# An elementwise add moved from GpSimd to an accumulating DMA, with a second buffer for its tile and VectorE's operations in another order

## The chip, the core and the metric

The kernel runs on one core of a Trainium2 chip. The metric is the time of one execution on the device in microseconds (us). It is given as the median of three runs, and a profiled execution shows where the time goes. The engines are TensorE (PE, with its weight loads as PEld), VectorE (DVE), ScalarE (ACT) and GpSimd (POOL); SyncE (SP) issues the loads and stores.

## The reference

128 samples of 64 channels and 1024 positions pass through four style-modulated 1-D convolutions with three taps (plain, upsampling by two, plain, downsampling by two), with blurs, and the input is added at the end:

```python
s = style @ mw.T + mb
weight = SCALE * w * s[:, None, :, None]
demod = lax.rsqrt(jnp.sum(weight * weight, axis=(2, 3)) + EPS)
weight = weight * demod[:, :, None, None]
...
x = x + _L0_cond_ref(x, cond_512, L0_cond_weights, ...)
```

All four layers and both blurs are linear, so each sample has one 64x64 filter with nine taps of its own, and a constant per channel. At the sequence's ends the four layers are done one by one (Ye, Ue, Ve, Oe).

## The kernel before, in words

Everything is float32. Two samples fill the 128 partitions; four samples make a quad, 32 quads in all. For each quad the kernel composes the nine taps on TensorE in stages (`stage1`, `stage2`, `stage3`, each with a scaled copy by ScalarE), and `combine_a` and `combine_b` on VectorE turn them into the filters `W` (tiles Wf) and `H` of a short convolution with five products. The nine-tap filter is three groups of three taps; the input's three planes, every third position each (344 columns), are combined into five inputs T0 to T4, and five products `conv0` to `conv4` (24 matmul instructions each, 340 columns) give three output planes.

The inputs of a quad, from its loaded tile X (both pairs of samples, three planes) and a work tile G of the same shape:

- `in_g2` (VectorE, line L712, 128x684) writes plane 2 of G, and `in_g01` (VectorE, L712, 128x1376) planes 0 and 1.
- `in1` (L776) writes T1 = plane 2 + plane 1 of G, `in2` (L781) T2 = plane 2 - plane 1. Both run on GpSimd from turn 1 on.
- `in04` (VectorE, L790, 128x1368) writes T0 and T4 from all three planes of G.
- `in3` (VectorE, L761) writes T3 from X alone.

G has one buffer, so the next quad's `in_g2` comes after all readers of the last quad's G. T tiles have two buffers, X two, and the PSUM pool `ps_w`, which the composing stages share, one. Y is a PSUM tile of its own; its spare columns also hold small sums of the constants, and a `memset` (L1524) clears them in turns 1 to 6 (`SMALL`).

The schedule is written out by hand: each engine runs its instructions in program order, and the tile framework adds the semaphores. After a set-up, four turns `early_turn(0)` to `early_turn(3)`, then `turn_of(q)` for q = 4 to 28, then the last quads in line. `turn_of(q)` works on several quads at once: it composes c = q + 2 (stages 2 and 3) and s = q + 4 (stage 1), ends the products of q and begins those of n = q + 1. Turn 4 is the entry (`entry`), with its own order. The products of a turn come in the order conv2(q), conv4(q), conv3(n), conv0(q), conv1(n) on TensorE. Between them:

- `r_sums` (L638, GpSimd) sums columns of the tile R that ScalarE has just copied out of stage2's PSUM.
- `sum2(q)` on VectorE (L712, Y from m and psA, then L862) follows conv2 and writes Y, on which conv4 accumulates; `sum1(n)` (L712, y from psA and m) follows conv1.
- `stage1_b(s)` has matmuls, then two operations of VectorE (L481, S from psS, one for each half), then a sum of S on GpSimd (L484).
- `share_sums` (L501) and `share_copy` (L529, ScalarE) prepare part of the next turn's stage2 in the `ps_w` bank; turn 5 is without them, and its stage2 is all matmuls (L589).
- `SIDE` and `LATE` hold side work of VectorE, one item a turn: set-up of tables and constants, and the sequence ends (for example `setup1`, L1016).

The profile's own lines name TensorE's matmuls by helper: L803 the products, L506 and L589 stage2, L621 stage3, L428 stage1, L1044 the ends, L1295 the constants.

Of the kernel before, what the change touches and what calls it, by code (L numbers as in the profile page):

```python
# [48 lines left out]
F32 = mybir.dt.float32  # L49
AF = mybir.ActivationFunctionType  # L50
ALU = mybir.AluOpType
# [12 lines left out]
def kernel(  # L64
# [10 lines left out]
    NP, P, NXC = x.shape  # L75
    B = 2 * NP
    NQ = B // 4
# [5 lines left out]
    nc_v, nc_a, nc_g = nc.vector, nc.scalar, nc.gpsimd  # L83
# [3 lines left out]
    const = ctx.enter_context(tc.tile_pool(name="const", bufs=1))  # L87
# [4 lines left out]
    wf_pool = ctx.enter_context(tc.tile_pool(name="wf_pool", bufs=3))  # L92
    tpool = ctx.enter_context(tc.tile_pool(name="tpool", bufs=2))
    mpool = ctx.enter_context(tc.tile_pool(name="mpool", bufs=1))
    gpool = ctx.enter_context(tc.tile_pool(name="gpool", bufs=1))
    opool = ctx.enter_context(tc.tile_pool(name="opool", bufs=2))
    ps_conv = ctx.enter_context(tc.tile_pool(name="ps_conv", bufs=2, space=PSUM))
    ps_w = ctx.enter_context(tc.tile_pool(name="ps_w", bufs=1, space=PSUM))
# [39 lines left out]
    PL = NXC // 3  # L138
# [27 lines left out]
    def unit(pool, name):  # L166

        if pool is ps_w:
            return [pool.tile([P, 512], F32, tag=f"u{r}", name=f"{name}_{r}") for r in range(2)]
        t = pool.tile([P, 2, 512], F32, tag="u", name=name)  # L170
        return [t[:, r, :] for r in range(2)]


    NB = 340
# [266 lines left out]
    def flat(t):  # L441
        return t.rearrange("c a o -> c (a o)")
# [117 lines left out]
    def stage2(q, pool=None, engs=(nc_a, nc_a), between=None):  # L560
        if q in shared_ps:
            ps = stage2_rest(q)
        else:
            ps = opened.pop(q, None)
            taps = range(9) if ps is None else range(3, 9)
            ps = stage2_taps(q, taps, ps or unit(pool or ps_w, f"psR{q}"))
        if between:
            between()
        t = r_pool.tile([P, 2, 9, C], F32, tag="R", name=f"R{q}")
        for r in range(2):  # L570
            scaled_copy(engs[r], flat(t[:, r, :7]), ps[r][:, : 7 * C], tC[:, q, r : r + 1])
        chain[q] = t
        return ps
# [28 lines left out]
    def tap(kind, g):  # L602
        return range(9)[TAPS[kind]][g]
# [32 lines left out]
    def r_sums(q, eng):  # L636
        t = chain[q]
        eng.tensor_add(t[:, :, 7:9], t[:, :, 2:6:3], t[:, :, 3:7:3])  # L638
# [97 lines left out]
    Ts = {}  # L736
    Gs = {}
# [5 lines left out]
    def plane(buf, i, pairs=BOTH_PAIRS):  # L743

        at = PL * (2 - i) if i < 3 else PL * 2 + 1
        return buf[:, pairs, at : at + NJ]
# [11 lines left out]
    def in3(q, pairs=BOTH_PAIRS):  # L758
        if q < NQ:
            X, t = Xs[q % NX], t_tile(q, "T3")  # L760
            nc_v.tensor_sub(t[:, pairs, 0, :NJ], plane(X, 3, pairs), plane(X, 1, pairs))  # L761

    def in_g01(q, pairs=BOTH_PAIRS):
        if q < NQ:
            X, g = g_tile(q)
            sum_of(g[:, pairs, PL:], X[:, pairs, : 2 * PL], 0.5, X[:, pairs, PL:], ALU.subtract)

    def in_g2(q, pairs=BOTH_PAIRS):
        if q < NQ:
            X, g = g_tile(q)  # L770
            sum_of(plane(g, 2, pairs), plane(X, 3, pairs), 0.5, plane(X, 2, pairs), ALU.subtract)

    def in1(q, eng):
        if q < NQ:
            t, g = t_tile(q, "T12"), Gs[q]
            eng.tensor_add(t[:, :, 0, :NJ], plane(g, 2), plane(g, 1))  # L776

    def in2(q, eng):
        if q < NQ:
            t, g = t_tile(q, "T12"), Gs[q]  # L780
            eng.tensor_sub(t[:, :, 1, :NJ], plane(g, 2), plane(g, 1))  # L781

    def in04(q, pairs=BOTH_PAIRS):
        if q < NQ:
            t, g = t_tile(q, "T04"), Gs[q]
            a, b = g[:, pairs, :NJ], g[:, pairs, 2 * PL : 2 * PL + NJ]
            both = lambda v, step: bass.AP(
                v.tensor, v.offset, [*(list(d) for d in v.ap[:-1]), [step, 2], [1, NJ]]
            )
            nc_v.tensor_sub(t[:, pairs, :, :NJ], both(a, PL), both(b, 1))  # L790

    def product(q, m, ps, groups=range(K), alone=False):

        W, H_ = Wq[q]
        tag, i = SLOT[m]
        for g in groups:
            for s, rows in enumerate(HALF):
                for c, cols in enumerate(HALF):
                    if m in (0, 4):
                        w = W[rows, tap(m // 2, g), c, :]  # L800
                    else:
                        w = H_[rows, m - 1, g, c, :]
                    nc.tensor.matmul(  # L803
                        ps[s][cols, :NB],
                        w,
                        Ts[q, tag][rows, c, i, g : g + NB],
                        start=(g == 0 and (m == 3 or alone)),
                        stop=(g == K - 1),
                        skip_group_check=True,
                    )  # L810
# [36 lines left out]
    def sum1(q):  # L847

        y1w[q] = m_tile("y1", q, 2)
        for s, a in parts(q):  # L850
            sum_of(y1w[q][:, s], a, 2.0, m3c[q][:, s])
# [4 lines left out]
    def sum2(q, steps=(0, 1)):  # L856
        if 0 in steps:
            m3 = m3c.pop(q)
            for s, a in enumerate(banks(q)):
                sum_of(Y[:, s, :NB], m3[:, s], 3.0, a[:, :NB])  # L860
        for s, a in parts(q) if 1 in steps else ():
            nc_v.tensor_sub(y1w[q][:, s], y1w[q][:, s], a)  # L862
# [4 lines left out]
    def conv0(q, *groups):  # L867
        product(q, 0, banks(q), groups)
# [18 lines left out]
            os[q][:, s, planes].rearrange("c i j -> c (i j)"),  # L887
        )


    raw = const.tile([P, 512], F32, name="raw")

    WIDE = 6
    ends_ps = {}
# [94 lines left out]
    g1 = const.tile([P, 6, C], F32, name="g1")  # L989

    Ye = [const.tile([P, HB, 8], F32, name=f"Ye{s}") for s in range(2)]
    Ue = [const.tile([P, HB, 11], F32, name=f"Ue{s}") for s in range(2)]
    Ve = [const.tile([P, HB, 12], F32, name=f"Ve{s}") for s in range(2)]
    Oe = const.tile([P, B, 3], F32, name="Oe")
# [33 lines left out]
    def setup1(part):  # L1028
        blurred(g1, woi[1], 0.25, 0.75, part)
# [248 lines left out]
    def high(n):  # L1278
        return Y[:, 1, NB + 4 : NB + 4 + n]
# [10 lines left out]
    def small(q):  # L1290
        l, bs = SMALL[q]
        dst = high(bs.stop - bs.start)
        src = c0f if l == 0 else cc[l - 1]
        for cols in HALF:
            nc.tensor.matmul(  # L1295
                dst[cols], wsum[T, l, :], src[T, bs], start=False, stop=True, skip_group_check=True
            )
# [26 lines left out]
    def last_factors():  # L1324
# [17 lines left out]
        11: lambda: add0(0),  # L1342
        12: lambda: add0(1),
        13: lambda: setup1(0),
        15: setup3,
        16: lambda: rest1_bias(0),
        17: lambda: rest1_bias(1),
# [7 lines left out]
        26: lambda: blur_side(0, 2),  # L1355
        27: lambda: blur_side(1, 2),
    }

    LATE = {13: lambda: setup1(1)}

    def extra(*at):
        EXTRA.get(at, lambda: None)()
# [1 line left out]
    def side(work, q):  # L1364
        work.get(q, lambda: None)()
# [117 lines left out]
    def turn_of(q):  # L1483
        n, c, s = q + 1, q + 2, q + 4
        entry = q == FIRST
        stage2(c)
        if entry:
            sum2(q)
            conv4(q)
            combine_a(n)  # L1490
            r_sums(c, nc_v)
        else:
            conv2(q)
            r_sums(c, nc_g)
            sum2(q)
            in2(n, nc_g)
        side(TABLES, q)
        for i in range(3):
            load(c + 1, slice(i, i + 1))
        stage3_b(c, open_a(n))  # L1500
        if entry:
            conv0(q, 0, 1)
        else:
            combine_a(n)
            conv4(q)
        stage3_a(c)
        combine_b(n)
        conv3(n)
        if entry:
            copy_m3(n)  # L1510
            stage1_a(s)
        outputs(q, 2)
        if not entry:
            if s < NQ:
                stage1_a(s)
            copy_m3(n)
        in04(n)
        if sharing(q):
            share_sums(c + 1)
        in_g2(c)  # L1520
        side(SIDE, q)
        if q in SMALL:
            l, bs = SMALL[q]
            nc_v.memset(high(bs.stop - bs.start), 0.0)  # L1524
        conv0(q, *((2,) if entry else range(K)))
        if entry:
            conv1(n, 0, 1)
        outputs(q, 1)
        if s < NQ:
            stage1_b(s)  # L1530
        in_g01(c)
        if sharing(q):
            share(c + 1, banks(q))
            share_copy(c + 1)
        outputs(q, 0)
        if q in SLOTS:
            matmuls, width, rest = SLOTS[q]
            slot(matmuls, width, Y_banks)
            rest()
        if s == NQ:  # L1540
            slot(ends3, 3, unit(ps_w, "psE"), 3)
            rest3()
        conv1(n, *((2,) if entry else range(K)))
        if q in SMALL:
            small(q)
        sum1(n)
        in3(c)
        side(LATE, q)
        if s == NQ:
            in04(c)  # L1550
        in1(c, nc_g)
        if s + 1 < NQ:
            scale3(s + 1)

# [3 lines left out]
        turn_of(q)  # L1558

    q, n, c = NQ - 3, NQ - 2, NQ - 1  # L1560
    stage2(c)
    conv2(q)
    in2(n, nc_g)
    stage3(c, 0)
    sum2(q, (0,))
    combine_a(n)
# [26 lines left out]
    q, n = NQ - 2, NQ - 1  # L1593
# [128 lines left out]
```

## Time and profile before

| | us |
|---|---|
| median of three runs | 475.28 |
| the three runs | 474.98, 475.28, 476.53 |
| span of the profiled execution | 475.5 |
| TensorE matmul, busy | 469.7 |
| VectorE, busy | 417.3 |
| ScalarE, busy | 312.0 |
| GpSimd, busy | 165.8 |

The profiled execution's own time is known only by its span, 475.5 us from the first to the last instruction. A timeline row reads: start, duration (of a merged group from the start of its first to the end of its last), engine, line, operation, output<-input, form, count, and in brackets the idle time before it with what ended it. A row of windows gives the stretch, its length, each engine's busy time with its number of instructions, the granted TensorE clock (1.00 is full), the busy share of the DMA engines and GB/s. A row of DMA issues gives the queue, the count, the size, and the median us from issue to landing.

### The profile page before, as it was taken

To read this page: it belongs to the slowest core of one execution; us is meant where nothing else is said; L and a number is where in the kernel's file an instruction comes from. 1 tells how busy PE (TensorE), PEld (TensorE's weight loads), DVE (VectorE), ACT (ScalarE), POOL (GpSimd) and SP (SyncE) were. 2 spreads that over 40 slices of the span, in tenths; PEclk is the share of its full clock that TensorE was granted. 3 is DMA by queue.
4 is the path that set the end of the run, shared out by engine and by line. 5 is a ranking of instruction groups with operands and counts; after the bars stand their busy time and mean duration, and the time that the engine had idled before them with its cause. 6 is when DMAs were issued, how large, how long until landed. Compare 5 with 4: busy or idle time off the path is not lost.

```text
span 475.5 us, 26771 instructions
## 1 busy us (share of the span) xinstructions
PE 469.7 (99%) x11932; PEld 349.5 (74%) x11932; DVE 417.3 (88%) x694; ACT 312.0 (66%) x711; POOL 165.8 (35%) x200
## 2 busy tenths in 40 slices
PE   9999999999999999999999999999999999999996
PEld 6987788777678876677776677766788787876653
DVE  3889998879989998899979899979998999999896
ACT  4565657577766676766667666667666777766464
POOL 3634033664444342233432233422333423243200
PEclk9999999999999999999999999999999999999999
DMA  5237456535445554345544454543555544455225
GB/s 176 71 115 224 150 151 180 152 113 177 139 145 166 166 166 136 123 150 169 163 150 126 130 168 152 178 124 121 152 164 169 164 145 147 148 152 161 80 91 193
DMA packets 52707, 70.71 MB, mean 149 GB/s; under 512 B 6000, under 2 KB 50672, under 8 KB 52592
## 3 DMA queue, kind: packets, MB, share of 16 engines
q1 hardware_dynamic: 52368, 68.78, 46.3%
q8 instruction: 93, 1.52, 1.4%
q10 hardware_dynamic: 224, 0.22, 0.1%
q14 instruction: 22, 0.18, 0.1%
HBM read 35.36 MB, written 33.62 MB: 145 GB/s over the span
## 4 chain that ended last, share of the span: by engine, by line
PE 99%; DVE 0%; ACT 0%; issue 0%
PE psA L803 47%; PE Y L803 12%; PE psR L506 9%; PE psW L621 7%; PE psA L621 7%; PE psS L428 6%; PE psR L589 5%; PE psA L506 2%; PE Y L1044 2%; PE Y L183 1%; PE Y L379 1%; PE psM L220 0%; PE psE L1044 0%; PE Y L255 0%; DVE o L882 0%; PE psM L255 0%
## 5 line engine op out<-in xcount | busy, mean ns | idle before, releaser
L803 PE MATMUL psA<-T,H 64*64 64x340 f32 x2304 | 185.9, 446 | 0.0
L803 PEld LDWEIGHTS psA<-T,H 64*64 64x64 f32 x2304 | 90.7, 133 | 46.9 <-issue 2.5
L712 DVE SCALAR_TENSOR_TENSOR G<-X 128x1376 f32<-128x1376 f32 (+2 forms) x65 | 78.0, 1206 | 0.2
L776 POOL TENSOR_TENSOR T<-G 128x684 f32<-128x684 f32 x28 | 46.3, 1652 | 73.7 <-DVE G L712 73.7
L484 POOL TENSOR_TENSOR S<-S 128x128 f32<-128x128 f32 x28 | 21.6, 772 | 139.7 <-ACT S L399 139.6
L399 ACT ACTIVATE R<-psR,tC 128x448 f32<-128x448 f32 x63 | 36.6, 631 | 43.6 <-PE psR L506 25.8
L803 PE MATMUL psA<-T,Wf 64*64 64x340 f32 x768 | 63.7, 446 | 0.0
L803 PE MATMUL Y<-T,Wf 64*64 64x340 f32 x768 | 62.4, 451 | 0.0
L712 DVE SCALAR_TENSOR_TENSOR Y<-m,psA 128x340 f32<-128x340 f32 x62 | 32.0, 516 | 28.2 <-PE psA L803 26.9
L399 ACT ACTIVATE psW<-psA 128x128 f32<-128x128 f32 x100 | 19.3, 268 | 49.1 <-PE psA L621 45.0
L790 DVE TENSOR_TENSOR T<-G 128x1368 f32<-128x1368 f32 (+1 forms) x33 | 50.8, 1541 | 0.0
L399 ACT ACTIVATE Wf<-psW,t 128x256 f32<-128x256 f32 (+2 forms) x76 | 32.7, 480 | 26.7 <-PE psW L621 26.4
L761 DVE TENSOR_TENSOR T<-X 128x684 f32<-128x684 f32 x32 | 47.7, 1492 | 0.0
L506 PE MATMUL psR<-S,E 64*64 64x64 f32 (+1 forms) x1472 | 46.8, 237 | 0.0
L781 POOL TENSOR_TENSOR T<-G 128x684 f32<-128x684 f32 x28 | 46.5, 1660 | 0.0
L428 PEld LDWEIGHTS psS<-wd,w2n 64*64 64x64 f32 x1120 | 35.1, 133 | 12.9 <-issue 0.3
L506 PEld LDWEIGHTS psR<-S,E 64*64 64x64 f32 x1472 | 39.5, 134 | 4.9 <-ACT psR L529 0.2
L803 PEld LDWEIGHTS Y<-T,Wf 64*64 64x64 f32 x768 | 30.3, 132 | 16.8
L803 PEld LDWEIGHTS psA<-T,Wf 64*64 64x64 f32 x768 | 29.8, 133 | 14.5
L880 ACT ACTIVATE o<-psA,tb,td 128x340 f32<-128x340 f32 x63 | 37.1, 648 | 5.0 <-PE psA L803 2.8
L880 ACT ACTIVATE o<-y,tb,td 128x340 f32<-128x340 f32 x62 | 38.5, 678 | 0.0
L880 ACT ACTIVATE o<-Y,tb,td 128x340 f32<-128x340 f32 x62 | 36.1, 639 | 2.8 <-PE Y L803 2.0
(180 smaller groups left out, 840.4 us busy)
## 6 DMA issues: line engine op xcount, KB each, us to landing
out<-o SPq DMA_DIRECT2D x191, 170.0 KB, 2.6
X<-in_x SPq DMA_DIRECT2D x150, 172.0 KB, 3.4
X<-in_x SPq DMA_DIRECT2D x14, 516.0 KB, 5.0
par<-in_params SPq DMA_DIRECT2D x3, 192.0 KB, 3.8
Xe<-in_x_ends SPq DMA_DIRECT2D x1, 512.0 KB, 4.5
out<-Oe SPq DMA_DIRECT2D x2, 96.0 KB, 2.1
out<-o ACTq DMA_DIRECT2D x1, 170.0 KB, 2.8
par<-in_params SPq DMA_DIRECT2D x1, 160.0 KB, 2.7
```

Of the source, the lines that this page charges most:

```text
L399: nc_a.activation(dst, src, AF.Copy, scale=f)
L428: nc.tensor.matmul(ps[r][cols, at * C : (at + n) * C], weight[rows], wd[c if r == 0 else 1 - c][rows, taps], start=first, stop=last, skip_ ...
L506: nc.tensor.matmul(dst[r][cols], weight[rows], st[c if r == 0 else 1 - c][rows, slots, :], start=False, stop=last, skip_group_check=True,)
L589: nc.tensor.matmul(ps[r][cols, lo * C : (lo + m) * C], E[rows, e + 2, :], src[rows, a, :], start=(n == 0), stop=(n == 8), skip_group_check ...
L621: nc.tensor.matmul(dst[r][cols], weight[rows], t[rows, c, slots, :], start=first, stop=last, skip_group_check=True,)
L712: nc_v.scalar_tensor_tensor(out, x, f, y, op0=ALU.mult, op1=op)
L761: nc_v.tensor_sub(t[:, pairs, 0, :NJ], plane(X, 3, pairs), plane(X, 1, pairs))
L776: eng.tensor_add(t[:, :, 0, :NJ], plane(g, 2), plane(g, 1))
L781: eng.tensor_sub(t[:, :, 1, :NJ], plane(g, 2), plane(g, 1))
L790: nc_v.tensor_sub(t[:, pairs, :, :NJ], both(a, PL), both(b, 1))
L803: nc.tensor.matmul(ps[s][cols, :NB], w, Ts[q, tag][rows, c, i, g : g + NB], start=(g == 0 and (m == 3 or alone)), stop=(g == K - 1), skip_ ...
L880: nc_a.activation(dst, src, AF.Identity, bias=add, scale=d3)
```

## The change

- G gets two buffers.
- A new `in1_dma(q)` replaces `in1` for quads 6 to 30. It issues a DMA from GpSimd's queue that adds plane 1 of G onto plane 2 in place, so T1 then lies in G itself, and conv1 of those quads reads it there (`first_of`). In a turn it is issued for n, behind `r_sums`. 
- `in2` moves from there to the end of the turn before, where `in1` was.
- `in04(n)` leaves the middle of the turn (but for the entry turn), and `in04(c)` stands at the end of each turn, between `sum1` and `in3`.
- `in_g2` and `in_g01` stand together, behind the side work and the memset, and ahead of stage 1's second half.
- `LATE` is gone: the second `setup1` is side work of turn 14.
- The tile `raw` lies over `Ye[0]` instead of having its own memory.
- In the last quads `in1_dma(30)` stands ahead of stage2, and `in2(30)` is gone from there.

```diff
-    gpool = ctx.enter_context(tc.tile_pool(name="gpool", bufs=1))
+    gpool = ctx.enter_context(tc.tile_pool(name="gpool", bufs=2))
...
+    def in1_dma(q):
+
+        g = Gs[q]
+        nc_g.dma_start(plane(g, 2), plane(g, 1), accum_op=ALU.add)
+        first_of[q] = g[:, :, :PL]
+
+    first_of = {}
+
...
+        if m == 1 and q in first_of:
+            src = first_of[q]
+        else:
+            src = Ts[q, tag][:, :, i]
...
-                        Ts[q, tag][rows, c, i, g : g + NB],
+                        src[rows, c, g : g + NB],
...
-    raw = const.tile([P, 512], F32, name="raw")
...
+    raw = Ye[0].rearrange("c b e -> c (b e)")
...
+        14: lambda: setup1(1),
...
-    LATE = {13: lambda: setup1(1)}
...
             r_sums(c, nc_g)
+            in1_dma(n)
             sum2(q)
-            in2(n, nc_g)
...
-        in04(n)
+        if entry:
+            in04(n)
         if sharing(q):
             share_sums(c + 1)
-        in_g2(c)
         side(SIDE, q)
         if q in SMALL:
             l, bs = SMALL[q]
             nc_v.memset(high(bs.stop - bs.start), 0.0)
+        in_g2(c)
+        in_g01(c)
         conv0(q, *((2,) if entry else range(K)))
...
         if s < NQ:
             stage1_b(s)
-        in_g01(c)
...
+        in2(c, nc_g)
         sum1(n)
+        in04(c)
         in3(c)
-        side(LATE, q)
-        if s == NQ:
-            in04(c)
-        in1(c, nc_g)
...
     q, n, c = NQ - 3, NQ - 2, NQ - 1
+    in1_dma(n)
     stage2(c)
     conv2(q)
-    in2(n, nc_g)
```

## The prediction

> **What bounds the kernel now.** I read the page's busy table and chain first, then the timelines of one late turn engine by engine, then the first turn of the late loop, then waits and DMA.
>
> ```profile
> span 475.5 us, 26771 instructions
> PE 469.7 (99%) x11932; PEld 349.5 (74%) x11932; DVE 417.3 (88%) x694; ACT 312.0 (66%) x711; POOL 165.8 (35%) x200
> PE 99%; DVE 0%; ACT 0%; issue 0%
> ```
>
> The chain that ended last is TensorE from end to end. So work taken off VectorE or GpSimd is worth nothing by itself, and the question is only whether some wait now reaches TensorE. TensorE's rows of turn 13 (first the end of turn 12, last the start of turn 14):
>
> ```profile
> 215.10 0.40 PE L506 MATMUL psR<-S,E 64*64 64x128 f32 x8
> 217.03 1.90 PE L803 MATMUL psA<-T,H 64*64 64x340 f32 x24
> 219.86 0.40 PE L621 MATMUL psA<-R,par 64*64 64x128 f32 x8
> 220.12 1.95 PE L803 MATMUL Y<-T,Wf 64*64 64x340 f32 x24
> 221.88 0.40 PE L621 MATMUL psW<-R,wsq 64*64 64x128 f32 x8
> 222.10 0.40 PE L621 MATMUL psW<-R,par 64*64 64x128 f32 x8
> 227.22 1.90 PE L803 MATMUL psA<-T,H 64*64 64x340 f32 x24
> 228.94 0.40 PE L506 MATMUL psR<-S,E 64*64 64x128 f32 x8
> ```
>
> 215.10 to 228.94 is one turn, 13.84 us: stage2, conv2 at 217.03, conv4 at 220.12, conv1 at 227.22. Back to back a product of 24 takes 1.72 (228.94 - 227.22). Eight of 64x128 go by in 0.22 (221.88 to 222.10), so behind those of 219.86 conv4 could start at 220.08; it starts 0.04 later and then takes 1.76 (221.88 - 220.12). That 0.08 is all that a turn could gain there.
>
> **The change, steady turns.** VectorE, GpSimd and one ScalarE row of the same stretch:
>
> ```profile
> 215.42 0.87 DVE L712 SCALAR_TENSOR_TENSOR y<-psA,m 128x680 f32<-128x680 f32 x1
> 216.21 1.81 DVE L761 TENSOR_TENSOR T<-X 128x684 f32<-128x684 f32 x1
> 219.00 1.07 DVE L712 SCALAR_TENSOR_TENSOR Y<-m,psA 128x340 f32<-128x340 f32 x2 [0.98 <-PE psA L803]
> 223.87 1.58 DVE L790 TENSOR_TENSOR T<-G 128x1368 f32<-128x1368 f32 x1
> 225.37 0.42 DVE L501 TENSOR_TENSOR S<-S 128x256 f32<-128x256 f32 x1
> 225.70 0.86 DVE L712 SCALAR_TENSOR_TENSOR G<-X 128x684 f32<-128x684 f32 x1
> 226.48 1.00 DVE L1016 SCALAR_TENSOR_TENSOR g<-par,g 128x192 f32<-128x192 f32 x2
> 227.41 0.60 DVE L481 SCALAR_TENSOR_TENSOR S<-psS,tB,S 128x128 f32<-128x128 f32 x2
> 227.92 1.58 DVE L712 SCALAR_TENSOR_TENSOR G<-X 128x1376 f32<-128x1376 f32 x1
> ```
>
> ```profile
> 215.64 1.65 POOL L776 TENSOR_TENSOR T<-G 128x684 f32<-128x684 f32 x1 [2.61 <-DVE G L712]
> 218.56 0.72 POOL L638 TENSOR_TENSOR R<-R 128x256 f32<-128x256 f32 x1 [1.27 <-ACT R L399]
> 226.05 0.82 POOL L484 TENSOR_TENSOR S<-S 128x128 f32<-128x128 f32 x1 [5.15 <-ACT S L399]
> ```
>
> ```profile
> 227.84 0.63 ACT L529 COPY psR<-psA 128x256 f32<-128x256 f32 x2
> ```
>
> Costs are start to start, since VectorE overlaps neighbours by some 0.08.
>
> *T0/T4 (in04, L790) out, first G part (in_g01, L712 128x1376) in, ahead of L481.* in04 is worth 225.37 - 223.87 = 1.50; in_g01 has the same 1.58 of duration, so 1.50 as well. So share_sums goes to 223.87, side to 224.20, in_g2 to 225.13, in_g01 to 225.91, and L481 stays at 227.41. That matters because L481 empties the PSUM bank that the copy L529 then fills for the next stage2: copy end 228.47 against stage2 at 228.94, 0.47 of cover. Net 0. L484 on GpSimd falls beside in_g01 now; at worst it holds VectorE for its own 0.82, and that is the one place where cover could run out by 0.35 in a turn; I take 0, since in_g01 starts first (225.91 against 226.05).
>
> *in04 ahead of in3, behind sum1.* sum1 waits for conv1: its end, 228.94, plus the 0.25 that sum2 shows behind conv2 (217.03 + 1.72 = 18.75, start 19.00), 229.19. Then 0.79 for sum1, in04 from 229.98 to 231.48, in3, and sum2 is due at 219.00 + 13.84 = 232.84. in3 has 1.36. It takes 1.81 now, beside GpSimd's add of in1; in turn 10, where other matmuls held sum1 back and that add was over:
>
> ```profile
> 188.52 0.86 DVE L761 TENSOR_TENSOR T<-X 128x684 f32<-128x684 f32 x1
> 191.32 1.07 DVE L712 SCALAR_TENSOR_TENSOR Y<-m,psA 128x340 f32<-128x340 f32 x2 [1.93 <-PE psA L803]
> ```
>
> At 0.86 it fits with 0.5 to spare; at 1.81 sum2, and conv4 behind it, are late by 0.45. GpSimd's in2 (1.65, the price of its twin L776) can start when in_g01 ends at 227.41 and L484 behind it at about 227.9, and ends at 229.55, before in04 at 229.98. So I take 0.86, and 0 for TensorE.
>
> *in1 as an accumulating DMA.* It leaves GpSimd's queue behind r_sums, at 218.56 + 0.72 = 219.28, with in2 and in04 of that quad done a turn's end before. Only the S sum at 226.05 queues behind it, which no one needs before the next turn. conv1 needs its 342 KiB at 227.22: 7.94 us. The second G buffer takes away the wait on conv1's reads. No DMA between SBUF tiles is in this trace, so bounds come from the loads:
>
> ```profile
> X<-in_x SPq DMA_DIRECT2D x150, 172.0 KB, 3.4
> out<-o SPq DMA_DIRECT2D x191, 170.0 KB, 2.6
> ```
>
> ```profile
> 221.28:222.28 1.00, 1.00 (x28) 0.70 (x24) 0.97 (x5) 0.72 (x2) 0.00 (x0) 1.00 0.90 279
> 222.28:223.28 1.00, 1.00 (x37) 0.73 (x32) 0.96 (x3) 0.35 (x1) 0.00 (x0) 1.00 0.10 37
> 224.28:225.28 1.00, 1.00 (x36) 0.77 (x32) 1.00 (x1) 0.69 (x3) 0.00 (x0) 1.00 0.08 31
> ```
>
> The second last column is the share of the DMA engines: full to 222.28 with the six X loads, then nearly idle. Low end 2.6 us, one store. High end: it starts only behind the X loads at 222.28, its three streams (two read, one written) cost three times two loads' bytes at 279 GB/s, 1.05 MB or 3.8 us, plus 3.4 to land: 229.5, which is 2.3 late. I take twice an X load, 6.8 us (the same rows of 1.4 KB, twice as many): 226.1, hidden by 1.1. [...]
>
> **The change, entry turn.** Turn 4 is different. Its VectorE rows:
>
> ```profile
> 96.37 0.87 DVE L712 SCALAR_TENSOR_TENSOR G<-X 128x684 f32<-128x684 f32 x1
> 100.74 0.14 DVE L1524 MEMSET Y<- 128x96 f32 x1 [2.39 <-ACT o L880]
> 100.79 0.53 DVE L481 SCALAR_TENSOR_TENSOR S<-psS,tB,S 128x128 f32<-128x128 f32 x2
> 101.23 1.58 DVE L712 SCALAR_TENSOR_TENSOR G<-X 128x1376 f32<-128x1376 f32 x1
> 102.73 0.86 DVE L712 SCALAR_TENSOR_TENSOR y<-psA,m 128x680 f32<-128x680 f32 x1
> ```
>
> ```profile
> 99.47 1.17 ACT L880 ACTIVATE o<-Y,tb,td 128x340 f32<-128x340 f32 x2
> ```
>
> ```profile
> 101.02 0.38 PE L1295 MATMUL Y<-c0f,wsum 64*64 64x96 f32 x4
> 101.21 2.71 PE L589 MATMUL psR<-S,E 64*64 64x192 f32 x70
> 103.92 1.88 PE L803 MATMUL psA<-T,H 64*64 64x340 f32 x22
> ```
>
> The memset of the spare columns of Y waits 2.39 us for ScalarE to have read Y (99.47 + 1.17 = 100.64). In before, L481 follows it directly, and TensorE's stage2 of turn 5 (L589) starts at 101.21, right behind L481's first half: it takes the very PSUM bank (pool ps_w, one buffer) that L481 reads. After the change, in_g2 and in_g01 both stand between memset and L481, behind a wait that does not move: in_g2 0.78, in_g01 102.73 - 101.23 = 1.50. L481 goes from 100.79 to 103.07, by 2.28, and L589 with it; its own slack is under 0.1, as it starts at 101.21 when the bank's half came free at about 101.1. **TensorE stalls 2.2 us, once.** Next late would be conv2 behind sum1, and sum2 of turn 5: sum1 then starts at 103.6, in04(6) at 104.4 (with in2 on GpSimd perhaps 104.8), in3 ends by 107.2, while conv2 (103.92 + 1.88 = 105.8 now) ends at 108.0. Covered. In turns 5 and 6 the memset comes after in04's slot and ScalarE's read of Y is over by then to within 0.1; 0.
>
> Nothing later gives the 2.2 back, as turns run at TensorE's pace. Sum on the profiled span: 475.5 + 2.2 = 477.7. The median of the runs, 475.28, lies 0.2 under that span; on it, 477.5. The other edits (raw laid over Ye, setup1's second half one turn later, the tail's one DMA) cost 0: the first only moves an address, and the others have work of several us ahead of whoever reads them.
>
> **The rivals.** (1) *The stall is paid back*: freed of in1's contention, VectorE is always ready, and conv4's loss of 0.08 per turn vanishes in 24 turns: -1.9, so 475.6, not slower. It decides from 0.035 a turn on. Against it: in turn 10 VectorE idled 1.93 before sum2 and the wait was still for TensorE's own conv2. (2) *TensorE does not depend on L481 there*, or the memset no longer waits: 475.3. Against: the bank and the 0.1 between the two rows. (3) *The DMA is late.* [...] It decides from 7.94 us after r_sums on, and each us late costs 24 (turns 5 to 28): 480 at 0.1 late, 502 at one, 561 at 3.5. [...] No run here shows such a DMA yet. (4) *in3 stays slow or L484 blocks in_g01*: 0.45 late in 24 turns, +11, 488 with the stall; it needs in2 to run past 229.98.
>
> **How the numbers follow.** My sum 0.62; paid back 0.13; no dependence 0.09; late DMA 0.10; slow in3 0.06. About 0.3% (1.4 us) is what a measurement can tell. Slower: 0.58 of my 0.62 (the 2.2 could shrink under 1.4) and both late cases, 0.74. Same: 0.21. Faster: 0.05, from rival 1 when it beats the stall. Range: the likeliest alone 476.7 to 478.4; down to 474.8 for rivals 1 and 2, up to 480 for a DMA late by 0.1 a turn; left out are the larger late cases and gains, under 0.2.
>
> **What would show it.** In the new trace: L589 of turn 5 waiting near 2 us for VectorE's L481; turns of 13.84 as before; L761 at about 0.86 in steady turns; no wait of conv1 for a DMA. Wrong if conv1 waits for G each turn, if sum2 starts without idle time and conv4 slides, or if turn 4 to 5 shows no gap.

## The result and the profile after

The changed kernel takes 482.23 us (median of 4 runs, 480.99 to 484.17), the kernel before 475.62 in the runs beside it: ratio 1.0138, 95% interval 1.0115 to 1.0161, or 6.6 us. It is slower, as predicted, but by three times the predicted 2.2 us. In every run of this study the time is 1.7 to 2.1 us above the span. Two executions that took far longer than all others (1733.79 us of the kernel before, 607.37 us of experiment 3) are left out of the ratios.

The page of the changed kernel: span, engines, and the chain that ended last.

```profile
span 481.2 us, 26775 instructions
...
PE 471.7 (98%) x11932; PEld 350.8 (73%) x11932; DVE 395.9 (82%) x694; ACT 311.6 (65%) x711; POOL 162.2 (34%) x200
...
PE 96%; DVE 2%; issue 1%; ACT 0%; DVEq 0%
```

VectorE was busy 21.4 us less (417.3 to 395.9). It has as many instructions as before (694); 20.0 us of the 21.4 are in3 (L761), whose 32 instructions took 47.7 us, most of them beside GpSimd's add, and take 27.7 now. That is worth nothing, since the chain was TensorE's before. New in the chain are 2% of VectorE and 1% of issue (time in which the engine waits for nothing that the profile shows). Most of both lies in turn 4, where the chain now runs through VectorE; the rest of the issue is TensorE's own. What each costs is found by comparing, turn by turn, when conv4 starts:

| stretch of the profiled execution | before, us | after, us | difference |
|---|---|---|---|
| start to conv4 of turn 4 | 91.08 | 89.81 | -1.27 |
| conv4 of turn 4 to conv4 of turn 5 | 15.89 | 19.93 | +4.04 |
| conv4 of turn 5 to TensorE's end | 364.00 | 366.93 | +2.93 |

The first line is the start of the program, which differs by up to 2.3 us between the profiles of this study. The other two are the loss: 4.0 us once, in the entry turn, and 2.9 us spread over the rest.

**The entry turn.** VectorE's and TensorE's rows of the timeline, and windows of 1 us with their granted clock (the number before the last two):

```profile
99.47 0.14 DVE L1534 MEMSET Y<- 128x96 f32 x1 [3.36 <-ACT o L892]
99.51 2.37 DVE L712 SCALAR_TENSOR_TENSOR G<-X 128x684 f32<-128x684 f32 x2
101.80 0.60 DVE L481 SCALAR_TENSOR_TENSOR S<-psS,tB,S 128x128 f32<-128x128 f32 x2
```

```profile
102.20 4.46 PE L589 MATMUL psR<-S,E 64*64 64x192 f32 x70 [2.07 <-DVE S L481]
```

```profile
102.00:103.00 1.00, 0.80 (x20) 0.73 (x24) 1.00 (x3) 0.44 (x1) 0.97 (x1) 1.00 0.97 318
103.00:104.00 1.00, 1.00 (x26) 1.00 (x20) 1.00 (x2) 0.00 (x0) 0.68 (x1) 0.59 0.66 116
104.00:105.00 1.00, 1.00 (x23) 1.00 (x20) 1.00 (x1) 0.00 (x0) 0.00 (x0) 0.50 0.94 234
105.00:106.00 1.00, 1.00 (x24) 1.00 (x20) 0.90 (x2) 0.00 (x0) 0.00 (x0) 0.50 0.06 14
```

The predicted stall stands there: memset, both parts of G (2.37), then L481, and L589 waits 2.07 us for it. But L589 itself then takes 4.46 us where it took 2.71, because the granted clock falls to 0.50 about 1 us after TensorE starts again; the trace gives that state 3.41 us. So the loss there is 2.07 for the wait and 4.46 - 2.71 = 1.75 for the half clock, 3.82 of the 4.04.

**A steady turn.** VectorE and GpSimd around conv4 at 223.00, then the DMA queues and issues:

```profile
219.08 1.57 DVE L798 TENSOR_TENSOR T<-G 128x1368 f32<-128x1368 f32 x1
220.57 0.86 DVE L761 TENSOR_TENSOR T<-X 128x684 f32<-128x684 f32 x1
221.88 1.07 DVE L712 SCALAR_TENSOR_TENSOR Y<-m,psA 128x340 f32<-128x340 f32 x2 [0.44 <-PE psA L815]
...
230.31 0.61 DVE L481 SCALAR_TENSOR_TENSOR S<-psS,tB,S 128x128 f32<-128x128 f32 x2
```

```profile
222.12 1.19 POOL L781 DMA_DIRECT2D G<-G  x1
228.94 1.77 POOL L484 TENSOR_TENSOR S<-S 128x128 f32<-128x128 f32 x1 [5.64 <-ACT S L399]
230.68 1.65 POOL L789 TENSOR_TENSOR T<-G 128x684 f32<-128x684 f32 x1
```

```profile
q0 software_dynamic: 6800, 8.76, 11.0%
q8 instruction: 93, 1.52, 1.5%
...
out<-o SPq DMA_DIRECT2D x191, 170.0 KB, 2.9
X<-in_x SPq DMA_DIRECT2D x150, 172.0 KB, 3.9
G<-G POOLq DMA_DIRECT2D x25, 342.0 KB, 6.3
```

in3 (L761) takes 0.86, VectorE still idles 0.44 before sum2, L481 keeps its place in the turn, and the DMA lands 6.3 us after issue with no wait of conv1. This turn lasts 13.84 us as before, and most do. A few do not: 14.15, 14.20, 14.23, 15.68. There TensorE stands still with nothing to wait for:

```profile
345.87 1.32 PE L815 MATMUL psA<-T,Wf 64*64 64x340 f32 x14
348.22 1.07 PE L815 MATMUL psA<-T,Wf 64*64 64x340 f32 x9 [1.03 <-issue]
```

**Where these gaps lie.** Queue q8, of the kind "instruction", moved 93 packets of 16,384 bytes, and TensorE has 23,994 recorded instructions, so a packet holds about 256 of them (experiment 4, with 64 instructions more, moved 94). Such a packet is called a fetch here. If they are numbered, the gap above is ahead of number 17,601, which is 193 modulo 256. So are the others that lengthen these turns, to within three: each is at the end of a block of 256, and TensorE goes on 1.3 to 1.6 us after a packet of q8 has ended. From the records:

```
              TensorE begins   fetch of the next block     TensorE begins
              the block at     starts at   took            the next block at
before        336.69           338.27      1.46            342.59
after         340.84           345.65      1.02            348.22
```

The next block is not asked for long ahead: in these two traces no fetch starts more than 0.9 us before TensorE begins the block ahead of it, and the medians lie 0.9 us (before) and 1.2 us (changed kernel) after that. In the last line it came 4.81 us after. The accumulating DMA and the six X loads share the engines there, as their issues show (4.38 is from the start of the first load's issue to the end of the sixth's):

```profile
339.93 1.19 POOL L781 DMA_DIRECT2D G<-G  x1
```

```profile
336.65 4.38 SPq L146 DMA_DIRECT2D X<-in_x  x6
```

The windows of that stretch (the column before the last is the busy share of the DMA engines; first the changed kernel, then the kernel before in the same part of its turn):

```profile
341.00:345.00 4.00, 4.00 (x85) 2.57 (x84) 3.90 (x10) 2.75 (x9) 0.11 (x1) 1.00 1.00 208
```

```profile
337.00:341.00 4.00, 4.00 (x88) 2.54 (x84) 3.90 (x9) 2.88 (x10) 0.72 (x1) 1.00 0.50 148
```

The gaps at block ends add up to 3.39 us in the changed kernel and 0.82 before: 2.57 of the 2.93. (They are counted from start to start, beyond the usual spacing; the gap shown above as 1.03 from the modelled end of the matmul before it counts about 1.4.)

### The profile page after: what moved, and what is told of

It is laid out like the page before. It is cut to its first block, busy times and chain, and to the rows that moved or that the text cites. A ratio compares the mean times of both kernels' runs of the same rounds, so it can differ in the third digit from the quotient of the medians.

```text
span 481.2 us, 26775 instructions
## 1 busy us (share of the span) xinstructions
PE 471.7 (98%) x11932; PEld 350.8 (73%) x11932; DVE 395.9 (82%) x694; ACT 311.6 (65%) x711; POOL 162.2 (34%) x200
## 4 chain that ended last, share of the span: by engine, by line
PE 96%; DVE 2%; issue 1%; ACT 0%; DVEq 0%
PE psA L815 45%; PE Y L815 12%; PE psR L506 9%; PE psW L621 7%; PE psA L621 7%; PE psS L428 5%; PE psR L589 5%; PE psA L506 2%; PE Y L1055 2%; PE Y L183 1%; DVE H L712 0%; DVE T L798 0%; PE psM L220 0%; DVE G L712 0%; PE Y L379 0%
## 5 line engine op out<-in xcount | busy, mean ns | idle before, releaser
L815 PE MATMUL psA<-T,H 64*64 64x340 f32 x1704 | 138.5, 447 | 0.0
L815 PEld LDWEIGHTS psA<-T,H 64*64 64x64 f32 x1704 | 68.4, 133 | 33.1 <-issue 1.4
L484 POOL TENSOR_TENSOR S<-S 128x128 f32<-128x128 f32 x28 | 30.3, 1083 | 151.5 <-ACT S L399 151.5
L712 DVE SCALAR_TENSOR_TENSOR G<-X 128x1376 f32<-128x1376 f32 (+2 forms) x65 | 76.9, 1221 | 0.3 <-issue 0.2
L712 DVE SCALAR_TENSOR_TENSOR y<-psA,m 128x680 f32<-128x680 f32 x31 | 26.9, 866 | 31.7 <-PE psA L815 27.4
L789 POOL TENSOR_TENSOR T<-G 128x684 f32<-128x684 f32 x28 | 46.6, 1665 | 14.0 <-DVE G L712 8.0
L815 PE MATMUL psA<-G,H 64*64 64x340 f32 x600 | 48.1, 446 | 0.0
L506 PE MATMUL psR<-S,E 64*64 64x64 f32 (+1 forms) x1472 | 47.8, 237 | 0.2
L638 POOL TENSOR_TENSOR R<-R 128x256 f32<-128x256 f32 x24 | 17.5, 729 | 88.6 <-DVE T L761 48.8
L506 PEld LDWEIGHTS psR<-S,E 64*64 64x64 f32 x1472 | 40.6, 134 | 5.0 <-issue 0.4
```

Source lines behind the costliest of these rows:

```text
L484: nc_g.tensor_add(t[:, :, 2], t[:, :, 2], t[:, :, 0])
L506: nc.tensor.matmul(dst[r][cols], weight[rows], st[c if r == 0 else 1 - c][rows, slots, :], start=False, stop=last, skip_group_check=True,)
L712: nc_v.scalar_tensor_tensor(out, x, f, y, op0=ALU.mult, op1=op)
L815: nc.tensor.matmul(ps[s][cols, :NB], w, src[rows, c, g : g + NB], start=(g == 0 and (m == 3 or alone)), stop=(g == K - 1), skip_group_chec ...
```

## The experiments

Times are medians; ratios are to the kernel before, run beside (475.84 to 476.32 us), with 95% intervals. "Gaps" are sums over each profile's turns 5 to 28: idle times of TensorE over 0.09 us at a block's end that end 1.1 to 1.65 us after a packet of q8.

**1. The entry turn's order put back.**

```diff
+        if entry:
+            in_g2(c)
         side(SIDE, q)
...
-        in_g2(c)
-        in_g01(c)
+        if not entry:
+            in_g2(c)
+            in_g01(c)
...
             stage1_b(s)
+        if entry:
+            in_g01(c)
```

> The changed kernel, but in turn 4 alone the old order of VectorE: in_g2 ahead of the side work, in_g01 behind stage1_b's two operations. Theory A (the wait of stage2 of turn 5 for L481, 2.1 us, and TensorE at half clock for 3.4 us after it, 1.75 us lost, together 4.0): 482.2 - 4.0 = 478.2 us, and no window of turn 5 with a granted clock under 1.00. The 2.6 us that are left are gaps of TensorE that no wait explains. Rival B (the DMA holds conv1 or steady turns are longer by VectorE's order): 481 or more, as both stay in.

479.26 us, 1.0078 (1.0058 to 1.0098): 0.6% less than the changed kernel, but 1.1 us more than expected. The wait for L481 and the half clock are gone. A new wait shows what the stall had covered:

```profile
102.39 2.55 DVE L798 TENSOR_TENSOR T<-G 128x1368 f32<-128x1368 f32 x1
104.86 1.39 DVE L761 TENSOR_TENSOR T<-X 128x684 f32<-128x684 f32 x1
106.17 1.05 DVE L712 SCALAR_TENSOR_TENSOR Y<-m,psA 128x340 f32<-128x340 f32 x2
```

in04 of quad 6 stands additionally between sum1 and sum2, takes 2.55 beside GpSimd's in2 (101.84 to 103.49), and conv4 waits 1.3 us for sum2. So a kernel without the stall still pays 1.5 us in this turn.

**2. The entry turn's order alone,** in the kernel before: `in_g2` and `in_g01` of turn 4 behind the memset, nothing else.

> The kernel before, with only turn 4 of VectorE changed: in_g2 and in_g01 behind the memset and ahead of L481. Theory A: 475.6 + 4.0 = 479.6 us, with an idle TensorE of 2.1 us before L589 and three windows of 1 us at clock 0.5. If the half clock were not a consequence of the idle time but of something else in the change: 475.6 + 2.2 = 477.8 us.

479.25 us, 1.0068 (1.0044 to 1.0091). L589 waits 2.07 us for L481, later turns are as before. The median is near the expected 479.6, but partly by luck: its profile shows no half clock, and turn 4 to 5 is 2.36 us longer, not 4.04. Its runs lie between 477.47 (mean clock 1.00) and 480.92 (0.996, which is what 3.41 us at half speed make of 481), and of the changed kernel's four runs the one without it is the fastest, 480.99: whether the half clock follows differs from run to run.

**3. GpSimd's add in place of the DMA,** on top of experiment 1:

```diff
-        nc_g.dma_start(plane(g, 2), plane(g, 1), accum_op=ALU.add)
+        nc_g.tensor_add(plane(g, 2), plane(g, 2), plane(g, 1))
```

> As the kernel with turn 4 in the old order, and the accumulating DMA replaced by a GpSimd add of the same two planes, in place and at the same position in its queue. Theory C (the rest of the loss, 2.6 us, is TensorE waiting for its own instructions while the DMA engines are full): 475.6 us, and the idle time put down to issue back at the level of before. Rival D (VectorE's and GpSimd's new order costs it): 478.2 us, as the order is the same.

477.36 us, 1.0031 (1.0018 to 1.0044). The sum2 wait in turn 5 stays; from there to the end it takes 363.63 us (before 364.00), with gaps of 0.45. So the new order costs nothing in steady turns, and the DMA, as the only difference to experiment 1, costs about 2 us (1.9 between the medians). Both theories missed the time, as neither had the 1.5 us of turn 5.

**4. TensorE kept busy in the stall:** 32 matmul instructions on zeros behind conv1 in turn 4, added into Y.

```diff
+        if entry:
+            keep_busy(8)
         in2(c, nc_g)
```

> The changed kernel with 16 matmuls of zeros (added to Y, 64x64 by 320 columns, about 2.1 us) put before stage2 of turn 5, where TensorE idles. Theory A: the idle time is filled, the clock stays at 1.00, L589 takes 2.7 and not 4.46 us: 482.2 - 1.75 = 480.5 us. If the slow L589 comes from VectorE's or GpSimd's work beside it: no change, 482.2 us.

479.72 us (480.5 expected), 1.0093 (1.0064 to 1.0123). L481 is as late as before, but the matmuls behind it run at full clock:

```profile
101.19 2.81 PE L602 MATMUL psR<-S,E 64*64 64x192 f32 x70
```

2.81 for 4.46 (L602 is L589 in this kernel's numbering). One profile would not show it, since the half clock also stays out in some runs with the stall. But none of the six runs has a mean clock under 0.998, while with the idle time in front three of four (changed kernel) and two of six (experiment 2) had 0.995 or 0.996. Without idle time in front, no half clock, in as many runs as were made.

**5 and 6. No stall at the entry, with the DMA and with the add.** Turn 4 in the old order, quad 6 by GpSimd's `in1`, its `in04` in turn 5; then the same with the add of experiment 3.

> The changed kernel from turn 6 on; turn 4 keeps the old order, quad 6 gets T1 from a GpSimd add as before, and its T0/T4 only late in turn 5, so that neither L481 (turn 4) nor sum2 (turn 5) is late. What is left is the steady turns and 24 accumulating DMAs. Theory C (instructions of TensorE arrive late while the DMA engines are full): 475.8 + 2.2 = 478.0 us, with idle time of TensorE put down to issue. Rival (the DMA costs nothing once turns 4 and 5 are mended): 475.6 us.

> The same with the accumulating DMA replaced by a GpSimd add in place. Theory C: no DMA, no loss: 475.5 us, as before, since its steady turns are as long as those of before (13.84 us). Rival D (VectorE's new order costs it): 478.0 us.

480.61 us, 1.008 (1.0058 to 1.0103), gaps 3.19; and 477.52, 1.0033 (1.0017 to 1.0049), gaps 0.44. Both are above what was expected (478.0 and 475.5), since I had not rid turn 5 of its cost: with two in04 in it, sum1 and sum2 are 0.9 and 0.5 us late and the turn is 1.8 us too long, in both kernels alike. The pair gives the DMA's price again, by itself: 3.1 us between the medians, 0.47%.

**7 and 8. A transfer that nobody reads, in the kernel before,** behind `r_sums` in turns 7 to 28: accumulating, then a plain copy.

```diff
             r_sums(c, nc_g)
+            if q > 6:
+                idle_dma()
             sum2(q)
             in2(n, nc_g)
```

> The kernel before, with one more DMA in each of turns 7 to 28, issued by GpSimd behind r_sums: it adds one plane of a scratch tile onto another, of the size of in1's, and nobody reads or waits for it. Theory C: 22 of 25 of 2.2, so 475.8 + 1.9 = 477.7 us, and the gaps of TensorE put down to issue. Rival F (the loss comes from conv1 waiting for the DMA or from reading G): 475.8 us.

> As the last, but a plain copy of the same bytes instead of the add. A store's packet of 1.4 KB takes about 60 ns of an engine and the accumulating one 128 ns, so theory C gives half: 476.7 us. If it is GpSimd's issuing of a DMA that costs, and not the DMA engines' time, it is as much as with the add: 477.7 us. Rival F: 475.8 us.

498.89 us, 1.0474 (1.0454 to 1.0495), and 489.08, 1.0272 (1.025 to 1.0294). Both missed by far, by another mechanism than the one I meant to test. GpSimd, VectorE and TensorE with the accumulating DMA, and the sum of TensorE's wait:

```profile
224.56 1.18 POOL L1000 DMA_DIRECT2D scratch<-scratch  x1
225.34 2.08 POOL L781 TENSOR_TENSOR T<-G 128x684 f32<-128x684 f32 x1
```

```profile
226.08 1.77 DVE L712 SCALAR_TENSOR_TENSOR H<-Wf 128x384 f32<-128x384 f32 x1
```

```profile
228.98 1.95 PE L803 MATMUL psA<-T,H 64*64 64x340 f32 x24 [0.81 <-DVE H L712]
```

```profile
PE psA L803 <- DVE H L712: 16.5, 21, 0.9
```

The issue takes GpSimd 1.18 us, so in2 behind it falls beside VectorE's first H step and holds it for 1.77 us where it took 0.57; H and conv3 are late every turn. The copy is issued in 0.72 and does it by less (H 1.30, conv3 0.34). In the changed kernel in2 stands a turn's end earlier, so nothing urgent is queued behind the issue; that this is what makes it harmless there is argued, not tested. The gaps in these two are small (0.65 and 0.24), though the accumulating DMA stands where the used one does, 0.9 us ahead of conv4. Fetches are late in both all the same (counted below). Every turn is longer here and TensorE waits for H in it, which may cover them; no run separates this.

**9 and 10. The unread transfer where nothing is queued behind it:** in the kernel of experiment 6, ahead of `r_sums`, plane 1 of G into an unused half of T12, accumulating and as a copy.

> The kernel that costs 477.5 (the add of T1 on GpSimd, the entry cost taken out; 1.0033) gets 22 accumulating DMAs of 342 KB that nobody reads, issued ahead of r_sums, with plane 1 of G as their source and an unused half of T12 as their target. Theory C (a transfer in this place crowds the DMA engines, TensorE's instruction fetches come late, and TensorE runs dry where a block of 256 instructions ends): it gains what the used DMA cost, 477.5 + 3.1 = 480.6, 479.0 to 482.5, with TensorE's extra idle time put down to issue. Theory D (the cost hangs on the result, on TensorE's reading of what a DMA has just written): 477.5, 476.5 to 478.3.

> As the one before, with plain copies in place of accumulating DMAs, whose packets took about half as long (59 ns for 128 ns). Theory C: about half of the 3.1 us, 479.0, 478.0 to 480.3. Theory D: 477.5. [...]

478.68 us, 1.0058 (1.0041 to 1.0075), and 481.13, 1.0115 (1.0094 to 1.0136), gaps 0.60 (in its fastest run) and 3.12. A transfer that nobody reads costs, so Theory D falls; the copy shows it, while the accumulating DMA's 1.2 us is at the edge of the noise. But the copy costs more than the accumulating DMA, 3.6 for 1.2, so the load by itself isn't the measure, and Theory C's doses were wrong. Two premises were off as well. The copy's packets were mostly of 4,104 bytes and took 188 ns, not 59; in all it kept the engines busy for about half as long as the accumulating DMA (80 such packets and 16 of 1,368 bytes at 60 ns, for 256 at 128 ns), and it costs more all the same. And the issue fell 5.1 us ahead of conv4, where the used DMA's falls 0.9 ahead, so this transfer ran in another stretch of the turn.

**11 and 12. A second accumulating DMA, and the X loads later,** both on the kernel of experiment 5.

> The kernel with the used DMA and without the entry cost (480.6) gets a second, unread accumulating DMA behind it in 22 turns. Theory C: the DMA engines are crowded for 12 us of a turn in place of 6, so at least as much again, 480.6 + 3.1 = 483.7, 482 to 487; no wait of conv1, since the used DMA is issued first. Theory D: 480.6.

> The kernel with the used DMA and without the entry cost (480.6), with the six loads of X issued behind the stores of the second output plane, so after the accumulating DMA has landed. Theory C: the stretch in which both run is gone, and most of the gaps with it, 478.2, 477.3 to 479.4. Theory D, or a cost of the DMA by itself: 480.6, 479.6 to 481.5.

482.99 us, 1.0133 (1.0097 to 1.0169), gaps 2.56 in its fastest run, conv1 without a wait: more, by 2.4 instead of 3.1, with intervals that still touch those of experiment 5. And 488.4, 1.0271 (1.0246 to 1.0297), gaps 10.33: the loads no longer meet the DMA, and it got worse by 7.8. So overlap of the two isn't needed. The idle time of TensorE's weight loads names the place:

```profile
PEld psA L621 <- issue: 8.4, 15, 1.0
```

L621 there is stage 3, ahead of conv4. In stages 2 and 3 the matmuls are small: before, one block passes there in 3.9 us (332.78 to 336.69), the next, mostly products, in 5.9 (to 342.59). The loads now run in that stretch.

**13 to 16. Loads away, and loads moved, with and without the DMA.** 13: the kernel of 5 without X loads from turn 7 on; 14: the same in the kernel before; 15: the kernel before, which has no accumulating DMA, with the later loads of 12; 16: the kernel of 5 with the loads behind `outputs(q, 2)`.

```diff
-        for i in range(3):
+        for i in range(3 if q < 7 else 0):
             load(c + 1, slice(i, i + 1))
```

> The kernel with the used DMA and without the entry cost (480.6), without the X loads from turn 7 on (what the last loads left in X is used again). Theory F (a block of instructions is fetched as a DMA packet of 16 KB that waits behind the transfers under way; it is late when loads, stores and the accumulating DMA keep the engines full): fetches start on time and the gaps go, 477.5, 476.3 to 478.5. Theory G (the accumulating DMA or its issue by GpSimd costs by itself): 480.6, 479.5 to 481.6.

> The control for the one before: the kernel before (475.9) without the X loads from turn 7 on. Theory F: only its own few gaps at block ends can go, 0.86 us in its profile, so 475.0, 474.3 to 476.0. Should it gain more than that, loads cost TensorE in another way than by late fetches, and the run before shows nothing about the DMA.

> The kernel before, without any accumulating DMA, its X loads issued behind the stores of the second output plane, as in the run of 488.4. Theory F with the place deciding (loads land in the stretch of small matmuls of stages 2 and 3, where 256 instructions pass in 3.5 to 4 us): gaps there without any such DMA, 480, 478 to 484, with idle time of TensorE put down to issue at L621 or L506. Theory G: 475.9, as the X tile is needed 7 us later still.

> The kernel with the used DMA and without the entry cost (480.6), its X loads issued behind the stores of the third output plane, at about conv3, so that they land during the long products. Theory F with the place deciding: no more than 480.6, I expect 479.5, 478 to 481. Were only the overlap with the accumulating DMA to count, it would be 480.6 or worse, as both still run together.

| run | us | ratio (interval) | gaps, us |
|---|---|---|---|
| 13 | 478.78 | 1.0044 (1.0032 to 1.0057) | 0.10 |
| 14 | 475.91 | 0.9990 (0.9979 to 1.0001) | 0.37 |
| 15 | 488.65 | 1.0275 (1.0246 to 1.0305) | 11.96 |
| 16 | 491.07 | 1.0303 (1.0278 to 1.0329) | 11.23 |

With all 24 accumulating DMAs but no loads, the gaps are gone and the ratio is that of the add (1.0033) within the intervals: Theory G falls. The profiles say it more sharply: from conv4 of turn 5 to TensorE's end, 13 takes 365.21 us and its control 363.48, and the 1.73 between them is what turn 5 costs (experiment 6 over the kernel before: 1.72). The control gains 0.4 us (by the interval 0 to 1.0), so loads cost little or nothing in another way. And the kernel before, without any such DMA, loses 12 us when only its loads are moved into the stretch of small matmuls. The windows of that stretch in 15, one of the gaps in TensorE's timeline, the sum of them in the waits, and the same stretch of the kernel before:

```profile
337.00:341.00 4.00, 3.58 (x117) 3.33 (x106) 2.96 (x4) 1.16 (x2) 2.70 (x3) 1.00 0.97 313
```

```profile
341.84 0.21 PE L621 MATMUL psA<-R,w0s 64*64 64x64 f32 x1 [1.25 <-issue]
```

```profile
PEld psA L621 <- issue: 9.3, 15, 1.4
```

```profile
332.00:336.00 4.00, 4.00 (x154) 3.25 (x149) 3.16 (x4) 2.51 (x5) 2.28 (x2) 1.00 0.63 182
```

The fetch of the block that begins at 341.84 started at 339.46, 2.94 us after TensorE had begun the block before at 336.52. Experiment 16 missed (479.5 expected): SyncE issued the loads where they stand in its program, behind two stores (228.10) and ahead of four (232.41), so they started only at 229.5 of a turn whose conv4 came at 223.9 and the next at 238.7, and loads and stores filled the small matmuls after all:

```profile
233.00:237.00 4.00, 3.86 (x138) 3.19 (x131) 3.47 (x4) 2.19 (x5) 0.81 (x2) 1.00 0.87 267
```

One count runs through all traces: of the 71 to 74 fetches between 105 and 455 us, how many start more than 2 us after TensorE began the block before.

| kernel | such fetches |
|---|---|
| before; entry order alone (2) | 5; 5 |
| new order with GpSimd's add (3; 6) | 4; 6 |
| new order with the accumulating DMA (changed; 1; 4; 5); with two (11) | 10; 9; 9; 12; 14 |
| unread transfer in the kernel before (7; 8); earlier in the turn (9; 10) | 11; 13; 8; 7 |
| without X loads: with the DMA (13); without (14) | 1; 0 |
| X loads in the small matmuls: with the DMA (12; 16); without (15) | 26; 14; 21 |

The DMA in its place makes fetches late (9 to 12, for 4 and 6 with the add), and so do loads in the wrong place (14 to 26); without the loads the DMA does not (1).

No version beat the kernel before. The gaps in its profile add up to 0.82 us, and keeping its fetches on time could gain no more.

## Why the prediction was right in direction and wrong in size

- *L481 in steady turns, net 0:* right. It starts 7.31 us after conv4 (230.31 - 223.00), 7.29 before.
- *in3 at 0.86 and sum2 with about 0.5 to spare:* right, 0.86 and 0.44; in2 ends at 232.33, 0.6 ahead of in04. L484 ran beside in_g01 as feared, but it was L484 that was held (1.77 for 0.82), not VectorE, whose two parts of G took 2.37 together, and it delayed no one.
- *The DMA lands in 6.8 us:* right, 6.3, and conv1 never waits. The accumulating DMA's packets of 1,368 bytes took 128 ns each, where those of the loads and stores (1,376 and 1,360 bytes) took 59 (all medians).
- *The DMA is hidden, 0 for TensorE:* this step failed. I took its cover, 7.94 us ahead of conv1, for the whole of its cost, and looked at the full DMA engines only for the DMA's own sake. They also bring TensorE its instructions (q8, 93 packets, 1.5% of the 16 engines' time), and its blocks of 256 came late. The term was put at 0 and measured 2 to 3 us (experiments 1 less 3: 0.47%; 5 less 6: 0.47%; gaps 2.57).
- *TensorE stalls 2.2 us, once:* the stall is right (2.07, in the predicted place, for the predicted reason), but the term was mis-sized, and this is the second step that failed. Behind the idle time TensorE ran at half clock for 3.41 us in the profile and, by their mean clocks (0.996 and 0.995), in two more of the four runs: 1.75 more, which experiment 4 takes away.
- *sum1, in04(6), in3 and sum2 of turn 5 are covered:* right with the stall, and only with it. Take it away and they cost 1.5 (experiment 1).
- *Nothing gives the 2.2 back:* right; rival 1 did not come: steady turns take 13.84 us as before, and VectorE's spare time stayed idle. Rival 2 falls with the wait, rival 3 with the landing, rival 4 with in3's 0.86. The 0.1 us late in every turn, on which the range's end of 480 and the chance of 0.10 stand, is shown by no run: GpSimd issued the DMA in 1.18 to 1.37 us, it landed 4.3 to 7.8 us after issue, and no conv1 waited for it. Whether VectorE's operations on two SBUF tensors hold such an issue back was not tested: 24 of the 25 issues ran beside sum2 and L874, which read PSUM and one SBUF tensor each, and only the last one began beside an operation on two SBUF tensors, in3, for 0.25 us of its 1.19.

Sum by the profile: 475.5 - 1.27 (start) + 2.07 + 1.75 + 0.22 (rest of the turn) + 2.93 = 481.2. Not settled is why a given fetch starts when it does: the traces don't show on which engine a packet of q8 waits, nor why the accumulating DMA of experiment 9, in much the same stretch as the copy of 10, hurt less. That transfers on the DMA engines make fetches late, and late fetches the gaps, is shown by the pairs with and without the DMA, by 13 and by 15; for each single gap it is argued. Nor is it shown why fetches as late as in 7 and 8 left few gaps.

## What to carry to other kernels

This kernel, bound by TensorE and full of small matmuls, reads its instructions through the same DMA engines as its data (q8, 93 packets of 16,384 bytes). In one like it, ask of a transfer not only whether its reader has it in time, but also whether the next block of instructions comes in time, and keep the stretch with the most instructions per microsecond clear (loads moved into it made the kernel before 2.75% slower, experiment 15). In the trace, idle time put down to issue, at equal distances in instructions (256 here), was the sign. And a short stall of TensorE should be priced with the half clock that may follow it (here 1.75 us behind a wait of 2.07, in some runs), and checked for what it covers: here, with it removed, the next wait appeared (1.3 us, for sum2).

## What the runs showed of the hardware

- A 2.07 us idle time of TensorE was followed by 3.41 us at clock 0.50 in the changed kernel's profile, and not in experiment 2's. By their mean clocks of 0.995 and 0.996 it followed in three of four and in two of six runs of these kernels.
- Fetches of about 256 instructions took 0.9 to 1.8 us in the trace before and 0.9 to 2.3 us in the changed kernel's. In the changed kernel TensorE went on 1.3 to 1.6 us after the end of one that it had stood still for.
- GpSimd needs 0.72 us to issue a 342 KB copy between tiles and 1.18 an accumulating one; an add queued right behind held VectorE's operation on two SBUF tensors from 0.57 to 1.77 us.
